# A four-stage Flamingo block on one core: the first slots' 1 / rms taken from their norm's variance, and the contexts' keys and values placed between layer 0's last block and its combinations

## The chip, the cores and the metric

The kernel runs on 1 core of one Trainium2 chip. TensorE (PE) multiplies 128x128 tiles into PSUM, VectorE (DVE) and ScalarE (ACT) do elementwise work and empty PSUM, GpSimd (POOL) does elementwise work on SBUF and issues the indirect DMAs, SyncE (SP) issues most other DMAs. Each engine works through its own instructions in order and waits on semaphores of the others.

The metric is the device time of one execution in microseconds. The kernel before took a median of 1169.84 us in 3 runs (1164.18 to 1171.93).

## The reference, cut to what matters

`x` is 4 x 512 x 256, the context `ctx` as well; all is float32. Four stages add to `x`: local attention with a feed-forward part, a mixture of 8 experts (two for each token), a slot attention against the context, and a second mixture of experts.

```python
x = x + tanh(g_xattn[0]) * aft_local_block(layernorm(x), ctx)
x = x + tanh(g_ffn[0])   * moe0(layernorm(x))          # layer 0 ends here
x = x + tanh(g_xattn[1]) * slot_attention(layernorm(x), ctx)
x = x + tanh(g_ffn[1])   * moe1(layernorm(x))

def layernorm(x, eps=1e-5):                  # mean 0, variance var / (var + eps)
    return (x - mean(x)) / sqrt(var(x) + eps)

def rmsnorm(x, w, eps=1e-6):
    return x * rsqrt(mean(x * x) + eps) * w

def slot_attention(slots, P):
    Pn = rmsnorm(P, input_norm_w)
    k, v = Pn @ Wk.T, Pn @ Wv.T              # once
    for _ in range(3):
        sn = rmsnorm(slots, slot_norm_w)
        scores = (sn @ Wq.T) @ k.T / 16
        attn = softmax(scores, axis=slots)
        attn = attn / (attn.sum(-1) + 1e-6)
        slots = gru_cell(attn @ v, slots)
    return slots
```

The slots of the first of the three iterations are the output of a layernorm without weights. Their mean square, which `rmsnorm` needs, is therefore `var * rs * rs` with the layernorm's own variance and `rs = (var + 1e-5) ** -0.5`.

## The kernel before

A batch is 512 tokens, four tiles (`NT`) of 128; D = 256 is two chunks (`ND`) of 128. A product of a batch with a 256-column weight chunk is a PSUM tile 128x512. Each float32 matmul of the program shows as two matmul instructions in the profile, a transpose as one.

Up to the end of the first iteration the order on PE, DVE, ACT and SP is the order of the code (`manual_schedule` over these engines, opened as `st_o` and closed behind `c1s(B - 1)`); POOL's order, and everything from there to the next such block, is laid out by a scheduler. `PSUM` is cut into four `mm` tiles, two `tr` tiles for transposes and two `tok` tiles.

**Start.** For batch 0 and 1 the code norms the inputs (`in_stats`, `in_apply`), adds the context, turns the sum (`in_turn`: eight transposes, evacuated as `embT`) and computes keys (`keys`: eight 128x512 matmul instructions from `embT`), queries and values. `window_turn()` transposes the position window `pw` and ends with the four transposes of `far`; behind it stand `in_turn(1)`, `more_emb(1)` (on POOL) and `keys(1)`. `spin(n)` (used at the start) multiplies the identity with itself into an `mm` tile that nobody reads: one 128x512 product for each n.

**Layer 0's experts.** `block(s)` runs 19 blocks of sorted rows; the last two are half blocks of 128 rows. Its order is: turn block s+1, `up()` of s, `down()` of s-1. `down()` multiplies `he` with the second weights, DVE copies the result to `yb`, SP stores it to `sorted_y`. After the loop `blocks[-1].down()` finishes the last one, and a branch on `more0` skips blocks that these inputs don't have. Context b is normed by ACT, POOL and DVE inside the loop (`ctx_norm`, `ctx_scale`).

**Hand-over.** `c0g(b)` issues eight indirect gathers (`got` from `sorted_y`) on POOL; `c0x(b, i)` adds the two gathered rows of token tile i to `x` on DVE (`combine`, two operations) and takes its statistics; after the fourth, `power()` computes `ve` on DVE and `rs` on POOL. For contexts 1 to 3: `ctx_turn(b)` (eight transposes; `pT`, one half evacuated by DVE, one by ACT), `ctx_keys(b)` (eight 128x512 matmul instructions; `kT`, one half by DVE, one by ACT), `ctx_values(b)` (two halves of eight 128x256 matmul instructions; the first copied by ACT, the second by DVE into `cs[b]`). The loads of `wih` and `whh` are issued by ACT.

**Slots, first iteration.** `c0n(b)` applies the layernorm (`s0`), `c0s(b)` transposes it (`hT`), `c1a1(b)` squares `hT` on ACT (tile `sq`, one buffer) and adds its two chunks (on DVE through `on_dve`, else on POOL), `c1a2(b)` sums over partitions with four 128x1 products against `ones` and takes the power -1/2 (`rsqrt4`: `ve` on DVE, the power on POOL), `c1b(b)` broadcasts the result by transposing it (`bp`, four transposes) and multiplies: `sn = hT * bp`. `c1s(b)` is scores, exp and division, `c1u1(b, b+1)` the update `u` with the combinations of the next batch between, `c1u2` its transposes, `c2(b)` the GRU: four gates g0 to g3 of eight matmul instructions each, then the new state, with other work called behind the gates.

Of the kernel before, what the change touches and what calls it, by code (L numbers as in the profile page):

```python
# [8 lines left out]
FP = mybir.dt.float32  # L9
# [56 lines left out]
def flamingo_kernel(  # L66
# [19 lines left out]
    def tr_tile():  # L86
        return ps_tr.tile([P, T], FP, tag="tr", name="tr")
# [147 lines left out]
    def rsqrt4(dst, src, mul, eps):  # L235

        ve = small.tile([P, NT], FP, tag="ve", name="ve")
        nc.vector.tensor_scalar(ve, src, mul, eps, ALU.mult, ALU.add)
        nc.gpsimd.tensor_tensor(dst, ve, mhalf, ALU.pow)
# [23 lines left out]
    def spin(n, width=T // P):  # L263

        sp = mm_tile()[:, : width * P]
        for _ in range(n):
            nc.tensor.matmul(
                sp.rearrange("p (a b) -> p a b", b=P), ident,
                ident.unsqueeze(1).to_broadcast([P, width, P]), start=True, stop=True,
            )  # L270
# [590 lines left out]
    def window_turn():  # L861
        def turned(*pairs):
            tp = tr_tile()
            for k, (i, j) in enumerate(pairs):
                nc.tensor.transpose(
                    tp[:, k * P : (k + 1) * P], pw[:, i, j * P : (j + 1) * P], ident
                )
            return tp

        def both(tp):  # L870
            return tp.rearrange("p (j t) -> p j t", j=2)

        act(ew[0][:, 0:2, :EDGE], both(turned((0, 0), (1, 0), (0, 1), (1, 1))))
        act(ew[1][:, 1:3, :EDGE], both(turned((2, 2), (3, 2), (2, 3), (3, 3))))
        tp = turned((1, 2), (2, 1))
        act(ew[0][:, 2, P:EDGE], tp[:, :P])
        act(ew[1][:, 0, :P], tp[:, P : 2 * P])
        tp = tr_tile()
        for i in TILES:
            nc.tensor.transpose(  # L880
                tp[:, i * P : (i + 1) * P], far[:, i : i + 1].to_broadcast([P, P]), ident
            )
        act(base, tp)
# [30 lines left out]
    def in_turn(b):  # L914
        a = A[b]
        embT = a["embT"] = ap.tile([P, ND, T], FP, tag="embT", name="embT")
        if b == 0:
            tps = [tr_tile() for _ in range(ND)]
            for i in TILES:
                if i == 2:  # L920
                    spin(1, 1)
                for c in range(ND):
                    nc.tensor.transpose(
                        tps[c][:, i * P : (i + 1) * P], a["emb"][:, i, c * P : (c + 1) * P],
                        ident,
                    )
            act(embT[:, 0, :], tps[0])
            dve(embT[:, 1, :], tps[1])
            spin(1, 1)
        else:  # L930
            transpose_tokens(embT, a["emb"], act)
# [279 lines left out]
    def ctx_scale(b):  # L1211
        rs = A[b]["rs"]
        for i in TILES:
            nc.vector.tensor_scalar(
                cs[b][:, i, :], cs[b][:, i, :], rs[:, i : i + 1], None, ALU.mult
            )
# [19 lines left out]
    values(0, 1, pool)  # L1236
    in_apply(1)
    window_turn()
    in_turn(1)
    more_emb(1, pool)  # L1240
    keys(1)
# [113 lines left out]
    def ctx_turn(b):  # L1355
        if b < 2:
            pT = ep2.tile([P, ND, T], FP, tag="pT", name="pT", bufs=2)
        else:
            pT = bp2.tile([P, ND, T], FP, tag="xn", name="pT")
        for c in range(ND):  # L1360
            tp = tr_tile()
            for i in TILES:
                nc.tensor.transpose(
                    tp[:, i * P : (i + 1) * P], cs[b][:, i, c * P : (c + 1) * P], ident
                )
            if c == 0:
                nc.vector.tensor_scalar(pT[:, c, :], tp, col("inw", c), None, ALU.mult)
            else:
                nc.scalar.activation(pT[:, c, :], tp, AF.Copy, scale=col("inw", c))
        return pT  # L1370

    def ctx_keys(b, pT):
        kT = kpool.tile([P, ND, T], FP, tag=f"kT{b}", name=f"kT{b}")
        for o in range(ND):
            kp = mm_tile()
            project(kp, [(feat(wkq, c, o), pT[:, c, :]) for c in range(ND)])
            if o == 0:
                nc.vector.tensor_scalar(kT[:, o, :], kp, col("snw", o), None, ALU.mult)
            else:
                nc.scalar.activation(kT[:, o, :], kp, AF.Copy, scale=col("snw", o))  # L1380
        kTs.append(kT)

    def ctx_values(b, pT):

        for g in range(NT // 2):
            vp = tok_tile()
            for k in range(2):
                project(
                    vp[:, k, :],
                    [  # L1390
                        (tokens(pT, c, 2 * g + k), wqkv1_t[:, 2 * ND + c, :])
                        for c in range(ND)
                    ],
                )
            (act, dve)[g](cs[b][:, 2 * g : 2 * g + 2, :], vp)
# [80 lines left out]
    for s in range(TOTAL0):  # L1476
        if s == TOTAL0 - 3:
            more0 = moe0.used(moe0.tab_half, 0)
        if s + AHEAD < TOTAL0:
            load_block(Block(*sure(s + AHEAD)))  # L1480
        block(s, 0, TOTAL0)
        if s == 1:
            moe0.blocks_behind()
        if s == 2:
            moe0.place(0)
        if s in (4, 8, 12):
            ctx_norm(s // 4)
        if s in (6, 10, 14):
            ctx_scale((s - 2) // 4)
    blocks[-1].down()  # L1490
    with tc.If(more0 < E, preferred_fallthrough_block=False):
        others = [(s,) for s in range(SURE0, PAIRS)]
# [27 lines left out]
    def c0x(b, i):  # L1520
        (got, n), norm = G[b][0][i], G[b][1]
        moe0.combine(got, b, i, n)
        norm.stats(xs[b], [i])
        if i == NT - 1:
            norm.power()

    c0g(0)
    pTs = {}
    pTs[1] = ctx_turn(1)
    ctx_keys(1, pTs[1])  # L1530
    ctx_values(1, pTs[1])
    pTs[2] = ctx_turn(2)
    c0x(0, 0)
    ctx_keys(2, pTs[2])
    c0x(0, 1)
    pTs[3] = ctx_turn(3)
    c0x(0, 2)
    ctx_keys(3, pTs[3])
    wih_t = load_w("wih_t", wih, queue=nc.scalar)
    whh_t = load_w("whh_t", whh, queue=nc.scalar)  # L1540
    c0x(0, 3)
    st_b.close()


    with ExitStack() as st_c:
# [4 lines left out]

        def c0n(b):

            s0 = bp1.tile([P, NT, D], FP, tag="xnT", name="s0")
            G[b][1].apply(s0, xs[b])
            G[b] = s0

        def c0s(b):

            if b:
                c0n(b)  # L1560
            s0 = G[b]
            hT = cp.tile([P, ND, T], FP, tag=f"hT{b}", name=f"hT{b}")
            transpose_tokens(hT, s0)
            hTs.append(hT)

        C, S = {}, {}

        def on_dve(b):
            c1a1(b, nc.vector)

        def c1a1(b, mix=nc.gpsimd):

            hT = hTs[b]
            sq = const.tile([P, ND, T], FP, tag="rows", name="sq")
            nc.scalar.activation(sq, hT, AF.Square)
            mix.tensor_tensor(sq[:, 0, :], sq[:, 0, :], sq[:, 1, :], ALU.add)
            S[b] = sq

        def c1a2(b):
            sq = S[b]  # L1580
            sp = tok_tile().rearrange("p a b -> p (a b)")[:, :NT]
            for i in range(NT):
                project(sp[:, i : i + 1], [(tokens(sq, 0, i), ones[:, 0:1])])
            rs = small.tile([P, NT], FP, tag="rs", name="rs")
            rsqrt4(rs, sp, 1.0 / D, 1e-6)
            S[b] = rs

        def c1b(b):

            hT, rs = hTs[b], S[b]  # L1590
            bp = tr_tile()
            for i in range(NT):
                nc.tensor.transpose(  # L1593
                    bp[:, i * P : (i + 1) * P], rs[:, i : i + 1].to_broadcast([P, P]), ident
                )
            sn = cp2.tile([P, ND, T], FP, tag="sn", name="sn")
            for c in range(ND):
                nc.vector.tensor_tensor(sn[:, c, :], hT[:, c, :], bp, ALU.mult)  # L1598
            S[b] = sn
# [396 lines left out]

        order = [b for it in range(ITERS) for b in range(B)]
        c0n(0)
        ctx_values(2, pTs[2])
        c0s(0)  # L2000
        c1a1(0, nc.vector)
        ctx_values(3, pTs[3])
        c1a2(0)
        c0g(1)
        c1b(0)

        adds = []
        for b in range(B - 1):
            c1s(b)
            for fn in adds:  # L2010
                fn()
            adds = []
            c1u2(b, c1u1(b, b + 1))
            c2(
                b, late=adds, g0=[(c0s, b + 1), (on_dve, b + 1)], g1=[(c1a2, b + 1)],
                g2=[(c1b, b + 1)] + ([(c0g, b + 2)] if b + 2 < B else []),
            )
        c1s(B - 1)
# [239 lines left out]
```

## Time and profile before

| | |
|---|---|
| median of 3 runs | 1169.84 us (1164.18 to 1171.93) |
| profiled execution | 1168.72 us, its span 1166.7 us |
| mean granted PE clock | 0.982 of full speed |
| last half block of layer 0 to the first scores of batch 0 | 400.6 to 431.2 us of the span |
| first iteration, batch 0 to the start of batch 3's scores | 431.2 to 554.4 us |
| combination of one tile on DVE (`combine`) | 2 x 480 ns |
| one indirect gather | 953 ns on POOL, 2.8 us to landing |
| power -1/2 of a 128x4 tile on POOL | 1.0 us |

In a timeline row stand: start in us of the span, duration, engine, line, operation, output<-inputs, how many are merged, and in brackets how long the engine had been idle before and what ended that. PE rows are matmuls, PEld rows weight loads. A window row gives the busy time and number of instructions of each engine in a stretch, then the TensorE clock that was granted (1.00 is full speed), the share of the DMA engines and what they moved.

### The profile page before, as it was taken

The numbers are of one execution on the slowest core, as the hardware profiler recorded it, in microseconds if no ns is written. First come the engines' busy times: TensorE is split into PE (matmuls) and PEld (weight loads), VectorE is DVE, ScalarE is ACT, GpSimd is POOL, SyncE is SP. The second block draws the span as 40 slices with busy tenths as digits, with TensorE's granted clock in tenths as the row PEclk, the third lists the DMA queues.
The fourth block names the chain that finished last, engine by engine and source line by source line (L and its number), as shares of the span: only waits on it lengthen the run. The fifth ranks groups of instructions, "written<-read, shape, count | busy, mean of one in ns | idle before, by whom it ended". The sixth has DMA issues, their size and how long they took to land.

```text
span 1166.7 us, 13509 instructions
## 1 busy us (share of the span) xinstructions
PE 1099.1 (94%) x4370; PEld 743.0 (64%) x4370; DVE 628.4 (54%) x1857; ACT 327.9 (28%) x625; POOL 289.2 (25%) x305
## 2 busy tenths in 40 slices
PE   7999999999989989999999999999998998999985
PEld 4757775766778755545555545554655486888874
DVE  7794974673534355644423332333466577666653
ACT  3132213131234223333324332433322222222211
POOL 5100113122300141441201211121131425433422
PEclk9999999999999999999999999999999999999998
DMA  9999401000178430110599200000010464867764
GB/s 318 370 340 342 163 1 50 23 4 33 57 234 265 158 105 17 34 36 1 123 215 214 55 0 1 1 1 0 1 38 9 153 220 148 271 199 250 246 209 149
DMA packets 122956, 147.41 MB, mean 126 GB/s; under 512 B 15076, under 2 KB 98082, under 8 KB 122880
## 3 DMA queue, kind: packets, MB, share of 16 engines
q1 hardware_dynamic: 114032, 127.25, 36.7%
q0 software_dynamic: 8160, 17.61, 4.5%
q10 hardware_dynamic: 688, 1.62, 0.4%
q8 instruction: 37, 0.61, 0.2%
q14 instruction: 39, 0.32, 0.1%
HBM read 76.74 MB, written 74.54 MB: 130 GB/s over the span
## 4 chain that ended last, share of the span: by engine, by line
PE 37%; DVE 11%; issue 6%; POOL 4%; DMA 3%; ACT 3%; POOLq 0%; ACTq 0%; DVEq 0%
PE mm L285 26%; PE tok L285 9%; DMA acc<-sorted_x,there 3%; POOL hT L1674 1%; POOL hT L1673 1%; PE tr L277 1%; DVE nb L1619 1%; POOL acc L1943 1%; DVE hT L1677 1%; ACT ex L1622 1%; DVE n L1693 1%; DVE x L744 1%; DVE vs L1610 1%; ACT n L1694 1%; DVE xn L254 1%
## 5 line engine op out<-in xcount | busy, mean ns | idle before, releaser
L285 PE MATMUL mm<-hT,whh_t 128*128 128x512 f32 x288 | 138.8, 601 | 0.0
L285 PE MATMUL mm<-uT,wih_t 128*128 128x512 f32 x288 | 135.7, 593 | 0.0
L285 PE MATMUL mm<-xT,gu 128*128 128x256 f32 (+1 forms) x672 | 132.1, 355 | 0.7 <-ACT xT L719 0.7
L285 PEld LDWEIGHTS mm<-xT,gu 128*128 128x128 f32 x672 | 115.7, 191 | 14.3 <-ACT xT L719 0.9
L285 PE MATMUL tok<-vs,ex 128*128 128x257 f32 x384 | 96.8, 398 | 12.4 <-DVE vs L1610 10.2
L285 PEld LDWEIGHTS mm<-uT,wih_t 128*128 128x128 f32 x288 | 54.5, 191 | 66.8 <-issue 65.6
L285 PEld LDWEIGHTS tok<-vs,ex 128*128 128x128 f32 x384 | 71.6, 195 | 38.7 <-ACT ex L1622 13.7
L285 PE MATMUL mm<-sn,kT 128*128 128x512 f32 x192 | 87.7, 611 | 1.6 <-DVE sn L1598 1.6
L285 PEld LDWEIGHTS mm<-hT,whh_t 128*128 128x128 f32 x288 | 52.7, 192 | 51.1 <-issue 50.8
L1926 ACT ACTIVATE sl<-mm,bias 128x256 f32<-128x256 f32 (+1 forms) x84 | 37.5, 448 | 158.1 <-PE mm L285 129.1
L285 PE MATMUL tok<-dn,h 128*128 128x256 f32 x296 | 71.5, 390 | 9.5 <-DVE h L1927 5.0
L824 POOL TENSOR_TENSOR rs<-ve,mhalf 128x4 f32<-128x4 f32 (+1 forms) x25 | 28.3, 1133 | 202.4 <-DVE ve L821 177.4
L285 PEld LDWEIGHTS mm<-sn,kT 128*128 128x128 f32 x192 | 37.6, 197 | 48.9 <-issue 39.8
L1673 POOL TENSOR_TENSOR hT<-hT,n 128x512 f32<-128x512 f32 x18 | 22.8, 1268 | 181.7 <-ACT n L1694 181.7
L285 PEld LDWEIGHTS tok<-dn,h 128*128 128x128 f32 x296 | 54.7, 194 | 20.1 <-DVE h L1927 8.6
L1988 POOL DMA_INDIRECT out<-acc,ids x37 | 37.8, 1022 | 98.5 <-DVE acc L1984 77.6
L1665 ACT ACTIVATE rz<-mm,brz 128x512 f32<-128x512 f32 x48 | 33.0, 687 | 96.0 <-PE mm L285 93.2
L1927 DVE SCALAR_TENSOR_TENSOR h<-mm,bias,sl 128x256 f32<-128x256 f32 (+1 forms) x84 | 37.7, 450 | 39.2 <-ACT sl L1926 37.7
L285 PE MATMUL mm<-aT,w_t 128*128 128x512 f32 x128 | 57.9, 609 | 0.9 <-ACT aT L1090 0.9
L285 PE MATMUL tok<-w_t,h1T 128*128 128x256 f32 x256 | 56.0, 379 | 0.0
L285 PEld LDWEIGHTS tok<-w_t,h1T 128*128 128x128 f32 x256 | 48.4, 190 | 6.9 <-issue 0.5
L1598 DVE TENSOR_TENSOR sn<-hT,tr 128x512 f32<-128x512 f32 x24 | 15.4, 683 | 64.0 <-PE tr L1593 64.0
(337 smaller groups left out, 1794.9 us busy)
## 6 DMA issues: line engine op xcount, KB each, us to landing
sorted_x<-zero SPq DMA_DIRECT2D x16, 1060.0 KB, 21.4
sorted_x<-zero SPq DMA_DIRECT2D x16, 1024.0 KB, 10.5
sorted_y<-zero SPq DMA_DIRECT2D x16, 1024.0 KB, 11.2
gu<-in_gate_w SPq DMA_DIRECT2D x21, 512.0 KB, 4.4
gu<-in_up_w SPq DMA_DIRECT2D x21, 512.0 KB, 5.6
dn<-in_down_w SPq DMA_DIRECT2D x21, 512.0 KB, 5.5
w<-in_w_stack SPq DMA_DIRECT2D x38, 256.0 KB, 3.6
xb<-sorted_x SPq DMA_DIRECT2D x17, 256.0 KB, 3.9
```

Source lines behind the costliest of these rows:

```text
L254: nc.vector.tensor_scalar(dst[:, i, :], src[:, i, :D], mean[:, i : i + 1], rs[:, i : i + 1], ALU.subtract, ALU.mult,)
L277: nc.tensor.transpose(tp[:, i * P : (i + 1) * P], src[:, i, c * P : (c + 1) * P], ident)
L285: nc.tensor.matmul(acc, lhsT, rhs, start=(k == 0), stop=(k == len(pairs) - 1))
L744: nc.vector.scalar_tensor_tensor(acc, got[:, 2 * n + k, :], self.w[b][:, k, i : i + 1], acc, ALU.mult, ALU.add,)
L824: pool.tensor_tensor(self.rs[:, part], self.ve[:, part], mhalf[:, part], ALU.pow)
L1598: nc.vector.tensor_tensor(sn[:, c, :], hT[:, c, :], bp, ALU.mult)
L1610: nc.vector.tensor_scalar(vs[:, j, 0:D], v[:, j, :], vs[:, j, D : D + 1], None, ALU.mult)
L1665: nc.scalar.activation(rz[:, g, :], gp, AF.Sigmoid, bias=brz[:, g : g + 1])
L1673: mix.tensor_tensor(h, h, n, ALU.subtract)
L1926: nc.scalar.activation(sl, hp[:, 0, :], AF.Silu, bias=bias[:, 0, f : f + 1])
L1927: nc.vector.scalar_tensor_tensor(self.h[:, f, :], hp[:, 1, :], bias[:, 1, f : f + 1], sl, ALU.add, ALU.mult)
L1988: ins = nc.gpsimd.indirect_dma_start(out=tokens_out, out_offset=bass.IndirectOffsetOnAxis(ap=self.ids[:, k : k + 1], axis=0), in_=acc[:, k ...
```

## The change

One product of the identity is put ahead of `in_turn(1)`. `ctx_turn(1)` moves from behind the branch to between the last two `down()`. The turns, keys and values of contexts 1 to 3 and the four combinations of batch 0 get a new order, and `ctx_values` can do one half at a time. In the first iteration the sum of squares is no longer computed: `c0n` takes 1 / rms from the layernorm's variance and `rs` (two products, `ve` and the power on 128x4 tiles). For batch 0, `c0first` broadcasts that before it transposes the slots, copies the broadcast to SBUF (`by`) and forms `sn` from the transposes in PSUM. For the other batches `c1a1` and `c1a2` fall away from g0 and g1 of the GRU before; `c1b` stays. Iterations 2 and 3 compute the sums as before.

```diff
     window_turn()
+    spin(1)
     in_turn(1)
...
-    def ctx_values(b, pT):
-
-        for g in range(NT // 2):
+    def ctx_values(b, pT, halves=range(NT // 2)):
+
+        for g in halves:
...
+    pTs = {1: ctx_turn(1)}
     blocks[-1].down()
     with tc.If(more0 < E, preferred_fallthrough_block=False):
...
     c0g(0)
-    pTs = {}
-    pTs[1] = ctx_turn(1)
     ctx_keys(1, pTs[1])
+    pTs[2] = ctx_turn(2)
     ctx_values(1, pTs[1])
-    pTs[2] = ctx_turn(2)
     c0x(0, 0)
     ctx_keys(2, pTs[2])
     c0x(0, 1)
     pTs[3] = ctx_turn(3)
     c0x(0, 2)
+    ctx_values(2, pTs[2])
+    c0x(0, 3)
     ctx_keys(3, pTs[3])
     wih_t = load_w("wih_t", wih, queue=nc.scalar)
     whh_t = load_w("whh_t", whh, queue=nc.scalar)
-    c0x(0, 3)
...
         def c0n(b):
+            norm = G[b][1]
+            q = small.tile([P, NT], FP, tag="q", name="q", bufs=2)
+            nc.vector.tensor_tensor(q, norm.mv[:, :, 1], norm.rs, ALU.mult)
+            nc.vector.tensor_tensor(q, q, norm.rs, ALU.mult)
+            rs = small.tile([P, NT], FP, tag="rs", name="rs")
+            rsqrt4(rs, q, 1.0, 1e-6)
+            S[b] = rs
             s0 = bp1.tile([P, NT, D], FP, tag="xnT", name="s0")
-            G[b][1].apply(s0, xs[b])
+            norm.apply(s0, xs[b])
             G[b] = s0
+        def c0first():
+            bp = tr_tile()
+            for i in range(NT):
+                nc.tensor.transpose(
+                    bp[:, i * P : (i + 1) * P], S[0][:, i : i + 1].to_broadcast([P, P]), ident
+                )
+            by = bp2.tile([P, T], FP, tag="relu", name="by")
+            act(by, bp)
+            hT = cp.tile([P, ND, T], FP, tag="hT0", name="hT0")
+            hTs.append(hT)
+            sn = cp2.tile([P, ND, T], FP, tag="sn", name="sn")
+            for c in range(ND):
+                tp = tr_tile()
+                for i in range(NT):
+                    nc.tensor.transpose(
+                        tp[:, i * P : (i + 1) * P], G[0][:, i, c * P : (c + 1) * P], ident
+                    )
+                nc.vector.tensor_tensor(sn[:, c, :], tp, by, ALU.mult)
+                act(hT[:, c, :], tp)
+            S[0] = sn
         def c0s(b):
-            if b:
-                c0n(b)
+            c0n(b)
...
-        def on_dve(b):
-            c1a1(b, nc.vector)
...
         c0n(0)
-        ctx_values(2, pTs[2])
-        c0s(0)
-        c1a1(0, nc.vector)
-        ctx_values(3, pTs[3])
-        c1a2(0)
+        ctx_values(3, pTs[3], [0])
+        c0first()
+        ctx_values(3, pTs[3], [1])
         c0g(1)
-        c1b(0)
...
             c2(
-                b, late=adds, g0=[(c0s, b + 1), (on_dve, b + 1)], g1=[(c1a2, b + 1)],
+                b, late=adds, g0=[(c0s, b + 1)],
                 g2=[(c1b, b + 1)] + ([(c0g, b + 2)] if b + 2 < B else []),
             )
```

## The prediction

> **What bounds the kernel now.** First the page: TensorE (PE) is busy for nearly the whole span, so only what changes its waits, its work or its clock can change the time.
>
> ```profile
> span 1166.7 us, 13509 instructions
> PE 1099.1 (94%) x4370; PEld 743.0 (64%) x4370; DVE 628.4 (54%) x1857; ACT 327.9 (28%) x625; POOL 289.2 (25%) x305
> ```
>
> The diff touches three stretches, so next the timeline of PE alone around the hand-over from layer 0 to layer 1 (start, us, engine, line, output<-inputs, count, the idle time before it and what ended it).
>
> ```profile
> 397.63 2.23 PE L285 MATMUL tok<-w,he 128*128 128x256 f32 x8
> 400.62 1.07 PE L1363 MATMUL tr<-ident,c 128*128 128x128 f32 x8 [0.76 <-PEq L1491]
> 402.09 3.70 PE L285 MATMUL mm<-pT,wkq 128*128 128x512 f32 x8 [0.41 <-DVE pT L1367]
> ...
> 427.38 0.95 PE L285 MATMUL tok<-ones,sq 128*128 128x1 f32 x8
> 429.73 0.65 PE L1593 MATMUL tr<-ident,rs 128*128 128x128 f32 x4 [1.41 <-POOL rs L239]
> 431.16 8.82 PE L285 MATMUL mm<-sn,kT 128*128 128x512 f32 x16 [0.78 <-DVE sn L1598]
> ```
>
> From 400.62 (first context transposes) to 431.16 (first scores) 30.5 us pass. Starts in the same timeline give the paces: 8 transposes 0.86 (453.64 to 454.51), 8 matmuls 128x512 3.44 (450.20 to 453.64), 16 matmuls 128x256 3.45 (405.63 to 409.08), 8 of 128x1 0.81 (457.95 to 458.76). The work of the stretch is, of the contexts 1 to 3, keys 10.3, values 10.3 and turns 2.6, slots' transposes 0.9, sums of squares 0.9, broadcast 0.4: 25.4. So 5.1 us are waits. And the 16 score matmuls, which take 6.87 in the next batch (473.01 to 479.88), take 8.66 here (431.16 to 439.82). Why, the windows view says (span, then busy us and instructions by engine, granted PE clock, DMA share, GB/s); I read it at both places where the diff takes away PE idle time.
>
> ```profile
> 24.00:26.60 2.60, 0.65 (x4) 0.41 (x4) 2.60 (x6) 1.25 (x4) 1.39 (x2) 1.00 1.07 364
> 26.60:28.60 2.00, 1.66 (x8) 0.94 (x8) 0.92 (x3) 0.59 (x2) 0.17 (x1) 0.95 1.12 334
> 28.60:30.00 1.40, 1.36 (x2) 0.84 (x3) 0.00 (x0) 0.48 (x1) 1.40 (x1) 0.50 1.10 347
> 30.00:32.00 2.00, 2.00 (x3) 0.68 (x2) 0.00 (x0) 0.00 (x0) 0.77 (x1) 0.54 1.10 346
> ...
> 427.00:431.00 4.00, 1.98 (x15) 1.60 (x13) 1.51 (x4) 0.00 (x0) 2.03 (x2) 1.00 0.00 0
> 431.00:433.00 2.00, 1.84 (x2) 0.84 (x3) 0.70 (x2) 0.00 (x0) 1.51 (x2) 0.55 0.32 84
> 433.00:434.50 1.50, 1.50 (x3) 0.67 (x2) 0.00 (x0) 0.00 (x0) 1.20 (x2) 0.50 0.35 117
> ```
>
> Behind each thinly used stretch PE gets half its clock for some 3.4 us, and the next four matmuls run at 0.86 instead of 0.43: 1.7 us each time.
>
> **A, spin(1) before in_turn(1).** PE is idle 1.63 us until 26.66 (waiting for DVE's emb), then has eight transposes paced by DVE, then keys(1) at half clock from 28.64 to 32.03. The spin is one 128x512 product, two matmuls, 0.86 us; it runs from about 25.0 to 25.9, inside that idle time, and delays nothing: its PSUM buffer was last used by keys(0), long evacuated. The 3.4 us from 25.0 to 28.4 then hold 1.7 us of work at the paces above instead of 0.85 (eight transposes). The 3.4 us from 7.9 on hold 1.7 (eight transposes, four matmuls of spin's 128x128, one 128x512) and kept the clock; those from 134.2 on hold 1.2 and kept it too, those from 813.5 on 1.3 and lost it, those from 171.8 on 0.8 and lost it: the limit is near 1.25. Gain: four matmuls, 1.7. Between 33.7 and 50 PE has no wait over 0.7, and up to 326 none on a DMA, so it is passed on. Bounds: 0 if the clock falls all the same, 1.7.
>
> **B, the hand-over.** (1) ctx_turn(1) now stands between the last two down() of layer 0. There PE waited 0.47 for DVE's he, so eight transposes (0.86) delay the last down by 0.4, and the first work behind the branch from 400.62 to 401.03; but that is now ctx_keys(1) itself, which started at 402.09. pT is ready: DVE evacuates it (0.75) between the two yb copies, ACT (0.69) in idle time. The last yb store slips on DVE by 0.4, but SP issued it only at 401.6, when the store before it had landed, and yb would be there at 400.7; so the gathers' start (404.47) doesn't move. What the branch itself costs (0.76) stays.
> (2) PE's queue is then keys 1, turn 2, values 1, keys 2, turn 3, values 2, keys 3, half of values 3, broadcast, slots' transposes, other half. Each evacuation now has a product to hide under, so the waits for pT (0.41, 0.57, 0.62 ahead of the three keys) go. Work: 3 keys 10.3, 2 turns 1.7, 3 values 10.3, broadcast 0.4, slots 0.9 = 23.6. From 401.03 that ends at 424.7 without waits.
> (3) The waits that replace the old ones. The gathers are issued 1.26 apart and land 2.8 later, the eighth at 416.2. On DVE the fourth combination stands behind values 2's copy: PE ends values 2 at 416.5, the copy runs to 417.4, the combination and its statistics (1.0+0.43+0.18) to 419.0, ve, POOL's power (1.05) to 420.3. New on DVE ahead of the four applies: q, q, ve, three 128x4 operations at 0.18 (as rd L1641 and L1642 follow each other at 448.65 and 448.81), 0.55; applies (1.38) to 422.3; beside them POOL's second power (1.01, row rs L239) to 422.0. PE has finished half of values 3 at 421.7, so the broadcast waits 0.4; the second block of slots' transposes needs the broadcast's PSUM buffer, which ACT's copy (0.58) frees: 0.4 more. Half of values 3 (1.7) covers DVE's two sn products (0.69 each). Scores start at 424.7+0.8 = 425.5 instead of 431.16: 5.7. Without the wait before, the clock stays up: 1.8 more. B is 7.5. Bounds: 4 (DVE 2 us later than I queue it, clock lost) and 8.3 (no wait at all).
> c0g(1)'s gathers come some 3 us earlier, now behind POOL's power, and batch 1's last lands near 438.5; its combination ran at 448.9, now 441.4. wih and whh move behind keys 3 on ACT, some 1 us later; they landed at 426 and are needed after 442.
>
> **C, the other three batches and iteration 2.** Each g1 loses ACT's square (1.06), DVE's sum (0.69) and eight matmuls 128x1.
>
> ```profile
> 457.95 0.95 PE L285 MATMUL tok<-ones,sq 128*128 128x1 f32 x8
> 458.76 1.96 PE L285 MATMUL mm<-hT,whh_t 128*128 128x512 f32 x4
> ...
> 537.24 1.88 PE L285 MATMUL mm<-uT,wih_t 128*128 128x512 f32 x4
> 539.24 1.05 PE L285 MATMUL tok<-ones,sq 128*128 128x1 f32 x8
> 540.15 1.96 PE L285 MATMUL mm<-hT,whh_t 128*128 128x512 f32 x4
> ```
>
> Batch 1 saves 0.8; batches 2 and 3, where PE also waited for the sums, 1.2 each (538.96, the end of the products before, to 540.15). q, q, ve delay the applies by 0.55: before they ended at 453.29 and the last transpose of the first four starts at 453.97, so no wait is made, by 0.1.
> What takes their place: in the changed program's order the squares of iteration 2 move up. Batch 0's stands on ACT between exp and u in batch 1's turn: u is 0.75 late, PE 0.5, but the last u waits for DVE's rd, which c0x sets, so nothing is passed on. Batch 1's stands between the third and fourth u of batch 2's turn, and its tile, single, is read by PE's sums behind the third u (529.3 to 530.1): square to 531.3, u to 531.8, PE's transposes at 531.8 instead of 530.61. That costs 1.2. In return the last batch's scores (554 to 571) lose eight 128x1 matmuls and a square that stood ahead of the last exp (562.32): 1.0. C: 0.8+1.2+1.2-1.2+1.0 = 3.0. Bounds 1.5 and 4.2.
>
> **The sum.** 1.7+7.5+3.0 = 12.2. The profiled run took 1168.7 (span 1166.7 and 2.0 around it), 1.1 under the median of the three (1169.84). So 1156.5 by the profile, 1157.6 by the median; I say 1157.
>
> **Rivals.**
> *The clock doesn't pay.* 3.5 of the 12.2 are two half-clock stretches. The clock falls in this profile at nine places before the end, and where it does depends on how the work lies in time; if the timed runs lose it at other places instead, 8.7 are left: 1160. For: the same kernel's runs spread from 1164.18 to 1171.93, more than its work can explain. Against: at both places idle time and transposes fill so much that most positions of a 3.4 us stretch are thin.
> [...]
> *The chain to the first sn.* Gathers, four combinations, power, q, power is now covered by only half of values 3. If DVE is 2 us later than queued above, PE waits that long and, with an idle stretch that thin, the clock goes too: 12.2-2-1.8 = 8.4, 1160.
> *Slower.* The first gather waited 24.19 us "until PE mm L285", an event at 404.1, by the profile. Its wait may be for a PE product behind the branch, whose place the change alters. If it had to wait for keys 3 (420.0), the gathers would land at 431.7, the combination end at 433.3, the applies at 436.6, scores start near 439.5 at half clock: 8.3 lost where 7.5 was to be gained, against A and C's 4.7: 3.6 slower, 1173. It turns the gain into a loss from a gather start of about 416 on (3.6 us earlier). Against: the last store's landing (403.55) explains the start as well, and the event belongs to keys 1, which come earlier.
>
> **Chances.** Forecast 0.60 (own range 1153 to 1160, from the bounds and the spread of a median); clock 0.24 and chain 0.12 (1157 to 1163); slower 0.04. 0.8 of it: 1152.5 to 1162.5. Over 1% faster is below 1158.1 (1% is about what a measurement of this kernel can tell): three quarters of the first case and a fifth of the next two, 0.52; within 1% 0.45; slower by over 1% 0.03.
>
> **What would show it.** Right: clock 1.00 at 26 to 32 and through the first scores; scores some 5.7+1.7 earlier; PE waits before the broadcast of 0.2 to 0.8; turns of batches 1 and 2 shorter by 0.8 and 1.2; a new wait of about 1.2 for u in batch 2's. Wrong: idle PE over 1.5 us before the broadcast, the gathers later than 404.5 less A, half clock at either place, or the gain of 408 lost again before 600.

## The result, and the profile after

The changed kernel took a median of 1162.42 us in 7 runs (1157.39 to 1164.09); beside them the kernel before took 1169.84 (7 runs, 1164.18 to 1171.93). The ratio is 0.993, with a 95% interval of 0.9906 to 0.9954. Two later comparisons, each on a chip of its own, gave 0.9897 (0.9873 to 0.9921) and 0.9922 (0.9888 to 0.9956). In microseconds of 1169.84 the three are 8.2, 12.0 and 9.1; their mean is 9.8, where 12.2 was forecast.

The page of the changed kernel says that the share of PE is the same, in a shorter span:

```profile
span 1160.2 us, 13466 instructions
PE 1098.6 (95%) x4340; PEld 742.3 (64%) x4340; DVE 624.8 (54%) x1860; ACT 324.9 (28%) x623; POOL 290.3 (25%) x305
```

The timeline of PE at the hand-over, changed kernel:

```profile
401.26 1.03 PE L285 MATMUL tok<-w,he 128*128 128x256 f32 x4
402.13 1.04 PE L1364 MATMUL tr<-ident,c 128*128 128x128 f32 x8
403.00 1.03 PE L285 MATMUL tok<-w,he 128*128 128x256 f32 x4
404.83 3.67 PE L285 MATMUL mm<-pT,wkq 128*128 128x512 f32 x8 [0.81 <-DVEq L1493]
...
426.23 0.65 PE L1570 MATMUL tr<-ident,rs 128*128 128x128 f32 x4 [0.47 <-POOL rs L239]
...
427.60 0.66 PE L1581 MATMUL tr<-ident,s 128*128 128x128 f32 x4 [0.28 <-ACT by L1574]
...
429.82 7.03 PE L285 MATMUL mm<-sn,kT 128*128 128x512 f32 x16
436.69 0.60 PE L285 MATMUL tok<-vs,ex 128*128 128x257 f32 x2
```

Before, the last two `down()` (they stand in one row) began at 397.63 and the first scores at 431.16, 33.5 later; now it is 401.26 (the context's transposes stand between the two) and 429.82, 28.6 later. From here on "last `down()`" in a stretch means the start of these two. The two waits that were forecast are there, 0.47 for POOL's `rs` and 0.28 for ACT's `by`. But the last two `down()` themselves begin 3.6 later than before, in a stretch where the diff changes nothing.

The windows view of the changed kernel at the places where the clock was looked at, and at a new one (columns as before: the granted clock is the third number from the right):

```profile
26.50:28.50 2.00, 1.99 (x9) 0.77 (x8) 1.65 (x5) 0.59 (x1) 0.00 (x0) 1.00 1.12 330
28.50:30.00 1.50, 1.20 (x7) 0.71 (x6) 0.00 (x0) 1.07 (x2) 0.95 (x1) 1.00 1.10 347
30.00:33.00 3.00, 3.00 (x8) 1.33 (x7) 1.01 (x3) 0.54 (x1) 1.40 (x1) 1.00 1.10 346
...
430.00:432.00 2.00, 2.00 (x6) 0.81 (x6) 1.03 (x3) 0.00 (x0) 0.34 (x1) 1.00 0.01 3
432.00:436.70 4.70, 4.70 (x13) 2.07 (x12) 3.17 (x10) 2.17 (x6) 3.53 (x4) 1.00 0.29 84
...
524.00:528.00 4.00, 2.43 (x19) 2.10 (x18) 3.76 (x11) 2.01 (x3) 1.39 (x2) 1.00 0.00 0
528.00:531.50 3.50, 3.50 (x6) 1.40 (x5) 2.23 (x9) 0.00 (x0) 2.71 (x3) 0.52 0.00 0
```

Keys of batch 1 and the first scores now have the full clock. The half clock at 528 is new; the stretch before it holds only 2.43 of PE in 4.00. The timeline of PE and that of ACT there:

```profile
523.99 0.49 PE L277 MATMUL tr<-ident,u 128*128 128x128 f32 x3
524.32 0.95 PE L285 MATMUL tok<-ones,sq 128*128 128x1 f32 x8
526.84 0.77 PE L277 MATMUL tr<-ident,u 128*128 128x128 f32 x5 [1.57 <-ACT u L1670]
```

```profile
525.37 1.06 ACT L1602 ACTIVATE sq<-hT 128x1024 f32<-128x1024 f32 x1 [1.56 <-PE tok L285]
526.33 0.46 ACT L1670 ACTIVATE u<-tok,rd 128x256 f32<-128x256 f32 x1
```

This is the wait forecast in C. ACT may write the next batch's square only when PE has read the last one (`tok<-ones,sq`), the fourth `u` stands behind the square, and PE waits 1.57 for it, at a place where it waited 1.19 for `u` before. The timeline of PE there in the kernel before:

```profile
528.93 0.49 PE L277 MATMUL tr<-ident,u 128*128 128x128 f32 x3
530.61 0.77 PE L277 MATMUL tr<-ident,u 128*128 128x128 f32 x5 [1.19 <-ACT u L1643]
```

From the start of the first three transposes of `u` to that of the last five 1.68 passed before and 2.85 now, so the wait costs 1.17, as forecast (1.2).

By stages the two profiled executions differ as follows (starts and stretches from the timelines of PE; low places are stretches of 3.41 us at a granted clock of 0.5, those at the very end left out; the first weigh is the first product of `ew`, at 33.74 before and 32.80 now, and the first `tok<-vs,ex` of a batch is its first u product):

| stretch | before | after |
|---|---|---|
| keys of batch 1: first transpose to first weigh | 7.08, 1 low | 5.52 |
| first weigh to the start of the last `down()` | 363.9, 2 low | 368.5, 5 low |
| last `down()` to the first scores | 33.5 | 28.6 |
| first scores to the first `tok<-vs,ex` | 8.66, 1 low | 6.87 |
| from there to the same of iteration 2's first | 143.6, 1 low | 141.1, 1 low |

The second row loses a part of what the other rows gain: it is 4.6 us longer with the same work and three low places more.

### The profile page after: what moved, and what is told of

Read it like the earlier page. It is cut to its first block, busy times and chain, and to the rows that moved or that the text cites. A ratio compares the mean times of both kernels' runs of the same rounds, so it can differ in the third digit from the quotient of the medians.

```text
span 1160.2 us, 13466 instructions
## 1 busy us (share of the span) xinstructions
PE 1098.6 (95%) x4340; PEld 742.3 (64%) x4340; DVE 624.8 (54%) x1860; ACT 324.9 (28%) x623; POOL 290.3 (25%) x305
## 4 chain that ended last, share of the span: by engine, by line
PE 36%; DVE 11%; issue 7%; POOL 5%; DMA 3%; ACT 2%; POOLq 0%; ACTq 0%; DVEq 0%
PE mm L285 25%; PE tok L285 9%; DMA acc<-sorted_x,there 3%; POOL acc L1970 1%; PE tr L277 1%; DVE nb L1646 1%; POOL hT L1701 1%; POOL hT L1700 1%; ACT ex L1649 1%; DVE n L1720 1%; DVE hT L1704 1%; ACT n L1721 1%; DVE vs L1637 1%; DVE xn L254 1%; DVE x L744 1%
## 5 line engine op out<-in xcount | busy, mean ns | idle before, releaser
L285 PE MATMUL mm<-sn,kT 128*128 128x512 f32 x192 | 84.5, 593 | 0.8 <-DVE sn L1625 0.8
L285 PEld LDWEIGHTS mm<-sn,kT 128*128 128x128 f32 x192 | 36.4, 190 | 46.0 <-issue 38.9
```

The lines of the kernel that those rows point to most:

```text
L285: nc.tensor.matmul(acc, lhsT, rhs, start=(k == 0), stop=(k == len(pairs) - 1))
```

## The experiments

**The spin alone.** The kernel before with

```diff
     window_turn()
+    spin(1)
     in_turn(1)
```

> The kernel before with spin(1) alone. Theory: the places of half clock depend on how the program's work happens to fall on a grid of 3.41 us, which lies differently in each execution, so each execution draws its own; a low place costs 1.7 us, and the spin takes away one thin place that nearly every position of the grid would hit. Then: keys of batch 1 (first transpose to first weigh) 5.4 to 5.6 instead of 7.08, at clock 1.00; first weigh to the last down() is 360.2 + 1.7 for each low place in it, whatever their number is this time; the rest of the program as before; time 1.6 faster, which a ratio of 0.9986 inside an interval that holds 1 would say. Rival: the spin itself costs the 4.6 us that the changed kernel lost between first weigh and the last down(): then that stretch is 368 here too, and without more than two low places in it; time 3 us slower. Rival: the half clock of 28.4 to 31.8 has nothing to do with how much PE does there: then keys take 7.08 as before.

Its timeline of PE:

```profile
25.53 1.02 PE L267 MATMUL mm<-ident 128*128 128x512 f32 x2
27.12 1.68 PE L277 MATMUL tr<-ident,emb 128*128 128x128 f32 x8 [0.57 <-DVE emb L910]
29.09 3.70 PE L285 MATMUL mm<-embT,wqkvo_t 128*128 128x512 f32 x8 [0.30 <-ACT embT L280]
```

Keys of batch 1 took 5.51 from first transpose to first weigh, at the full clock. First weigh to the start of the last `down()` took 368.1 with four low places, against 367.0 by 360.2 + 4 x 1.7. The stretch was long here too, but with four low places, where the rival that the spin itself costs the time allowed no more than two; whether it is the spin that brings them, the repeats below say. Time: 0.998 (0.9951 to 1.0008), nothing that can be told.

**The order alone.** Contexts and combinations in the new order, `ctx_turn(1)` moved, but the sums of squares as before and no spin. Against the changed kernel:

```diff
         c0n(0)
         ctx_values(3, pTs[3], [0])
-        c0first()
+        c0s(0)
+        c1a1(0, nc.vector)
         ctx_values(3, pTs[3], [1])
+        c1a2(0)
         c0g(1)
+        c1b(0)
```

> The changed order of contexts and combinations alone (ctx_turn(1) between the last two down(), turns ahead of values, values 2 behind the third combination, values 3 in two halves), with the old sums of squares for the first 1 / rms and in the loop, and no spin. Theory: the order by itself saves the three waits for pT (0.41, 0.57, 0.62) and half a turn, about 2.5, and gives back about 1.7, since the squares and their sums of batch 0 have only half of values 3 to hide under: last down() to the first u product 42.19 before, here 40.5 to 42 with one low place in it (PE waits over 1 us remain before the sums and the broadcast), 38.8 to 40.3 without. The batch turns as before (40.1, 40.7). Time 1 faster, not to be told from before. Rival (the two parts of the hand-over add up, and the order is most of the 6.8): 36 to 38.

Its timeline of PE:

```profile
426.77 1.89 PE L285 MATMUL tok<-wqkv_t,pT 128*128 128x256 f32 x8
429.76 1.02 PE L285 MATMUL tok<-ones,sq 128*128 128x1 f32 x8 [1.10 <-DVE sq L1577]
432.19 0.65 PE L1594 MATMUL tr<-ident,rs 128*128 128x128 f32 x4 [1.41 <-POOL rs L239]
433.62 6.62 PE L285 MATMUL mm<-sn,kT 128*128 128x512 f32 x8 [0.78 <-DVE sn L1599]
```

From the last `down()` to the first u product it took 41.95, with two low places in a row behind these waits (scores to u product 9.89, 3.0 more than at the full clock). Without the clock that is 38.9, against 40.4 before (42.19 less 1.79): the order by itself is worth 1.5 here. Ratio 0.9992 (0.9972 to 1.0013).

**1 / rms from the variance alone.** The order of before, no spin. Against the kernel before:

```diff
         ctx_values(2, pTs[2])
-        c0s(0)
-        c1a1(0, nc.vector)
+        c0first()
         ctx_values(3, pTs[3])
-        c1a2(0)
         c0g(1)
-        c1b(0)
```

and the same `c0n` and the same calls in the loop as in the changed kernel.

> 1 / rms from the variance alone, for all four batches, with the order of contexts and combinations of before, and no spin. Theory: at the hand-over it saves the sums (0.81) and the waits of 1.41 and 0.78, since values 2 lies ahead of the broadcast and values 3 behind it: 42.19 to about 39 with a low place in the scores, 37.4 without one. Together with the order alone (about 1) less than the 6.8 of both: the order pays in full only with the shorter chain. Batch 1's turn 0.9 shorter, batch 2's 1.0, batch 3's not shorter, since the square's wait for PE's sums delays the fourth u by 1.2 (a wait of about 1.6 ahead of the transposes of u), longer by 1.7 where the clock falls behind it; last scores 0.8 shorter. Time 5 to 7 faster, ratio about 0.995. Rival (parts add up): 36 or less at the hand-over if the order alone gives less than 1, and the loop's saving the whole 3.0.

```profile
428.78 0.65 PE L1569 MATMUL tr<-ident,rs 128*128 128x128 f32 x4 [0.53 <-POOL rs L239]
...
430.15 0.66 PE L1580 MATMUL tr<-ident,s 128*128 128x128 f32 x4 [0.28 <-ACT by L1573]
430.64 3.62 PE L285 MATMUL tok<-wqkv_t,pT 128*128 128x256 f32 x16
434.10 6.17 PE L285 MATMUL mm<-sn,kT 128*128 128x512 f32 x14
```

This is its timeline of PE: the waits of 1.41 and 0.78 are gone, 0.53 and 0.28 have come, and the scores follow the values with no low place. Last `down()` to the first u product: 38.12 (37.4 was expected). That is 2.3 under the 40.4. Order 1.5 and variance 2.3 make 3.8; both together make 5.0 (40.4 to 35.43), so 1.2 comes only from the two together. The batch turns (from the first u product of one batch to that of the next) are those of the changed kernel, 39.16, 39.73 and 42.33, the half clock behind the wait for `u` included (at 532.2). Ratio 0.9967 (0.9939 to 0.9994), 3.9 us where 5 to 7 were expected.

**The same two kernels once more.** No edit.

> The kernel before once more, for a second look at its clock. Theory (a free grid of 3.41 us, and half clock for the stretch of it that follows one filled less than about 0.38): the low places will not all be those of the first look (28.4, 175.2, 250.3, 431.2, 574.5, 816.9, 888.6, 902.2, 1127.5); with the grid at another phase some of them go and others come (9, 132, 174 twice, 294, 324, 972), all of them behind thin stretches, and first weigh to the last down() is 360.2 + 1.7 for each low place in it. Rival (the clock falls at fixed places of the program): the same nine places within 0.5 us, 363.9 again.

> The changed kernel once more. Theory: low places differ from those of its first look (9.3, 173 twice, 251.6, 299.4, 330.1, 528.1, 811.4, 883.1, 896.7 twice, 1122.0), and the stretch from first weigh to the last down() differs from 368.46 by 1.7 for each place more or fewer; what does not hang on the clock comes again to 0.1: keys 1 start 3.57 behind the last down(), waits of 0.47 and 0.28 at the broadcast, 1.57 ahead of the transposes of u in batch 2's turn. Ratio to before 0.991 to 0.996. Rival (fixed places): 368.4 again, with all places as they were.

The kernel before had low places at 27.9, 174.7 (two in a row), 253.2, 301.0, 324.8, 437.5, 580.8, 823.2, 908.5, 976.8, 993.9 and 1133.8 (two). From first weigh to the last `down()` there were five, not two, and it took 369.4, not 363.9; 360.2 + 5 x 1.7 is 368.7. One product shows it, `shared_in(3)`: the timeline of PE in the first execution, and then that in the second.

```profile
296.30 2.22 PE L285 MATMUL tok<-rw,xnT 128*128 128x8 f32 x16 [0.24 <-ACT xnT L280]
298.38 7.11 PE L285 MATMUL mm<-xnT,ws 128*128 128x512 f32 x16
```

```profile
297.99 2.22 PE L285 MATMUL tok<-rw,xnT 128*128 128x8 f32 x16 [0.24 <-ACT xnT L280]
300.06 8.81 PE L285 MATMUL mm<-xnT,ws 128*128 128x512 f32 x16
```

The program is the same, what stands ahead of it is the same, and its sixteen matmuls take 1.70 more. So the places are not fixed, and the spin isn't needed for a stretch of 369. That it is the execution and not only the chip, the runs of the third comparison show: of 19 executions of the kernel before on one chip, the one with the lowest mean granted clock (0.973) took 1175.78 us, and the three with the highest (0.985) 1163.97 to 1164.83. The changed kernel, once more, had again five low places there (172.5 twice, 251.0, 298.8, 322.7; one of them elsewhere than at first) and 369.4; what does not hang on the clock came again: keys 1 3.44 behind the last `down()` (3.57 at first), 28.4 from the last `down()` to the scores, 1.57 ahead of the transposes of `u`, turns of 39.16 and 39.73. The ratio, 0.9897, is a little below the range given, 0.991 to 0.996.

**The spin taken out of the changed kernel, beside the changed kernel.**

> The changed kernel, beside the next two on one chip. Theory: the work that the change takes off the path is the same each time (hand-over 32.9 to 33.1 from the last down() to the first u product, turns 39.16, 39.73, 42.3), 7.4 in all, and what the clock adds or takes differs from execution to execution; ratio to before between 0.990 and 0.994. Rival (its ratios of 0.993 and 0.9897 were two different gains on two chips): outside 0.989 to 0.995.

> The changed kernel without spin(1). Theory: half clock in the keys of batch 1 is a matter of the grid's phase and comes in most executions without the spin (three of four so far) and in none with it (six so far): keys of batch 1 5.5 to 7.1 here, first transpose to first weigh, 6.4 in the mean; the spin is worth about 1, less than the 1.7 forecast and less than can be told by time: 0 to 2 us over the changed kernel. Rival (the spin is worth its 1.7 each time): 7.08 here. Rival (it is worth nothing): 5.5 here, and no low place within 24 to 32.

Without the spin, the timeline of PE:

```profile
26.93 2.02 PE L277 MATMUL tr<-ident,emb 128*128 128x128 f32 x8 [1.26 <-DVE emb L910]
28.91 4.99 PE L285 MATMUL mm<-embT,wqkvo_t 128*128 128x512 f32 x8
```

6.80 from first transpose to first weigh, with a low place at 28.1. The changed kernel beside it had 5.52 and hand-over and turns as before (28.57, 39.17, 39.73, 42.33); its ratio, 0.9922, is inside the range given. Without the spin the ratio is 0.9941 (0.9914 to 0.9968), and the medians are 2.1 us apart (1161.43 and 1159.29); the intervals overlap, so the time doesn't tell what the spin is worth. Of the five traces of kernels without the spin four have a low place there, and the stretch took 7.08, 6.74, 6.42, 5.52 and 6.80, 6.51 in the mean; with it none of eight has one, and all show 5.51 or 5.52.

**The sum of squares in a tile of its own.** The changed kernel with

```diff
             nc.scalar.activation(sq, hT, AF.Square)
-            mix.tensor_tensor(sq[:, 0, :], sq[:, 0, :], sq[:, 1, :], ALU.add)
-            S[b] = sq
+            sm = const.tile([P, T], FP, tag="sqs", name="sm")
+            mix.tensor_tensor(sm, sq[:, 0, :], sq[:, 1, :], ALU.add)
+            S[b] = sm
```

and the products against `ones` read `sm`. It ran three times:

> The changed kernel, and the sum of the two squares goes to a tile of its own, so that the single square tile is held until the sum is taken and not until PE has read it. Theory: what batch 3's turn lost (33.83 before to 35.48 from the first u product of batch 2 to the first sn,kT product) is the square's wait for PE's sums and the low clock that the wait's thin stretch brings: here the stretch is 32.3 to 32.8, the wait ahead of the transposes of u 0.9 to 1.1 instead of 1.57, no low place within 524 to 532; the rest as in the changed kernel; time 1.2 to 2.9 under it, ratio to before 0.990 to 0.992. Rival (the wait is for something else, u or rd itself): the wait stays at 1.5 and the stretch at 33.8 or more; time as the changed kernel.

> The changed kernel with the sum of squares in a tile of its own, once more and timed in more rounds. What does not hang on the clock comes again: no wait ahead of the transposes of u in batch 2's turn, the four and a half later batch turns 38.06 and not 38.52. These make 1.57 + 5 x 0.46 = 3.9 against the changed kernel, and 1.7 more where the clock fell behind the wait at 528: ratio to before 0.988 to 0.992. Rival (its first time was low because its clock fell less by chance): 0.992 or more.

> The changed kernel with the sum of squares in a tile of its own, on the same chip as the changed kernel. Theory: turns 39.16, 39.73, 39.67 (42.3 before it) and 38.06 in place of 38.52: 2.6 + 5 x 0.46 = 4.9, less what the clock gives back, so 3 to 6 us under the changed kernel. Rival (no difference, as the medians 1163.46 and 1163.78 on one chip say): within 1.5 us.

Its timelines of PE and ACT at the place of the new wait:

```profile
521.05 0.49 PE L277 MATMUL tr<-ident,u 128*128 128x128 f32 x3
521.38 0.95 PE L285 MATMUL tok<-ones,sm 128*128 128x1 f32 x8
522.32 0.76 PE L277 MATMUL tr<-ident,u 128*128 128x128 f32 x5
```

```profile
516.00 1.06 ACT L1602 ACTIVATE sq<-hT 128x1024 f32<-128x1024 f32 x1 [1.82 <-DVE hT L1705]
516.96 0.45 ACT L1671 ACTIVATE u<-tok,rd 128x256 f32<-128x256 f32 x1
```

The square now stands ahead of the four `u`, not between the third and the fourth, and PE does not wait for `u` at all; 0.9 to 1.1 was expected to be left. The third turn (first u product of batch 2 to that of batch 3) is 39.67 in all three traces, where the changed kernel has 42.33 with the half clock, and 40.64 in the kernel without the spin, whose clock fell elsewhere. From the first u product of batch 2 to the last batch's scores it is 32.8, at the upper end of what was expected. In iteration 2 the square has moved one exp forward, and four turns are 38.06 instead of 38.52. The whole first iteration (first u product to that of iteration 2) takes 138.6 in two traces and 140.3, with a low place at 570, in the third, instead of 141.1; the next six turns take 227.8 instead of 229.6. In time: 0.9893 (0.9862 to 0.9924), 0.9867 (0.9843 to 0.9892) and 0.9909 (0.9876 to 0.9942), in the two sessions that timed the changed kernel too it is under it both times, by 0.0030 and 0.0013 (medians 1163.46 to 1163.78, and 1157.35 to 1159.29). The first two ratios are lower than expected, and the last difference, 1.9, lies between the two theories. The work saved is shown; that the time follows is likely, but no interval excludes that it doesn't. Against the kernel before it is faster by about 1%.

**Throwaway products in the thin stretches.** The last kernel with five more calls: `spin(1)` ahead of `moe_turn(1)`, ahead of `moe_turn(2)` and between `c1u2(3, u)` and `d0b1(2, act)`, `spin(2)` ahead of the first `blocks[0].turn()`, and

```diff
+                spin(4)
                 others()
```

> The kernel with the sum of squares in a tile of its own, and nine throwaway products of 128x512 more (0.86 us each, 7.7 of added work on PE) in the thin stretches that every trace so far shows: one ahead of moe_turn(1), one ahead of moe_turn(2), two ahead of the first block's turn, one between c1u2(3) and d0b1(2), four ahead of the late blocks' branch. Theory: they stand where PE waits anyway (0.43, 0.43, 1.65, 0.98, 4.47), so the work costs 1 to 1.5 us, and takes away the low places behind these stretches, 3 to 5 in an execution at 1.7: time 4 to 6 us under the kernel without them, ratio to before 0.984 to 0.987; no low places near 174, 250, 329, 890 and 1108. Rival (the granted clock does not follow what PE does there): low places stay and the time is 1 to 3 us more.

The gain did not come: 0.9872 (0.9847 to 0.9897) beside 0.9867 without them. Nor did most of the low places go: behind the targets they stood at 174.5, 249.6 and 1123.4, and only that near 890 was gone (near 329 this chip's traces have none, with the products or without). Three of the places were read wrongly. Ahead of the late blocks, in its timeline of PE, and then in that of the same session without the products:

```profile
1114.26 0.38 PE L715 MATMUL tr<-ident,xn 128*128 128x128 f32 x2
1114.48 3.60 PE L267 MATMUL mm<-ident 128*128 128x512 f32 x8
1122.05 2.48 PE L285 MATMUL tok<-dn,h 128*128 128x256 f32 x8 [3.98 <-issue]
```

```profile
1122.35 2.67 PE L285 MATMUL tok<-dn,h 128*128 128x256 f32 x7 [4.59 <-issue]
```

Without them PE stood 4.59 at that branch; with 3.44 of products it stood 3.98 behind them. In the twelve traces without them it is 3.90 to 4.59, so nothing shows that they hid any of it; it looks as if the wait at this branch starts when PE gets there. And the thin stretch near 172 is made by the sixteen 128x8 products: PE counts as busy for 2.2 us with them, but the low place behind stayed (174.5), although the spin in front of it ran; so did that behind the next such products (249.6). Ahead of the first block, at last, PE had nothing to wait for on this chip, since it had waited earlier (last section), and two products more simply took 1.7. Two low places in a row near 174 became one, and 8 were left where the same session's trace without the products has 11. But the other two traces without them have 7 and 10, so this one doesn't show that the products kept the clock; the 7.7 us of work bought nothing that the time shows.

## Why the prediction came out as it did

The first median, 1162.42, is inside the range (1152.5 to 1162.5) by only 0.08. It is above the forecast's own 1153 to 1160 and among the times of its two milder rivals, and a gain of under 1% had been given 0.45, less than the 0.52 of a larger one. Where one median falls in so wide a spread is luck: by the mean gain of 9.8 it would be 1160.0. The mechanism of each step was seen; most of the sizes were too large. Term by term, from the stretches above:

| step | forecast | measured |
|---|---|---|
| A: keys of batch 1 at full clock | 1.7 | 1.0 (6.51 to 5.52, means) |
| B: order and waits, to the first scores | 5.7 | 5.0 (33.53 to 28.56) |
| B: clock in the first scores | 1.8 | 2.3 (9.18, mean of four traces; 6.87) |
| C: three turns, without the clock | 3.0 | 2.7 (142.06 to 141.09 less 1.7) |
| C: clock behind the new wait | 0 | -0.4 (1.7 x (3/4 - 5/5)) |
| sum | 12.2 | 10.6 |

The sum lies between the three timed gains, 8.2, 9.1 and 12.0.

**A** was "four matmuls, 1.7", each time. In these traces a low place follows a thin stretch of the 3.41 us grid on which the clock changes (last section), and without the spin the grid still missed it in one trace of five; also, when the low place comes early, part of it falls on transposes that wait for `emb` anyway (26.5 in the kernel with the order alone, 6.42). So it is 1.0 in the mean. The limit "near 1.25" did not follow from its rows, of which 1.2 kept the clock and 1.3 lost it; thirteen traces show a band from 1.2 to 1.4 in which both happen (last section). The spin, with 1.7, is clear of it.

**B**, order and waits: keys 1 began 3.57 behind the last `down()` (forecast 3.40), and from there to the scores 24.99 passed (24.5). The waits named are the right ones, 0.47 and 0.28 for 0.4 and 0.4; the rest is a tenth here and there between groups that the sum of the paces doesn't hold. One reading was wrong: the 0.47 that PE was to have waited for the last `down()` is the idle time of the weight loads (`[0.47 <-DVE he L1178]` in PEld's row at 398.72); PE's matmuls began there only 0.23 later than their pace, so the transposes hide under less of it. The 33.53 is the first execution's. In the second, on the chip of the second comparison, it was 34.52, since PE waited 1.61 for the third context's `pT`, where it had waited 0.62 (415.88):

```profile
422.34 3.70 PE L285 MATMUL mm<-pT,wkq 128*128 128x512 f32 x8 [1.61 <-DVE pT L1367]
```

The changed kernel has no wait ahead of these keys in any of its traces, so B was worth about 6 there, and part of that comparison's 12.0 may be this; one trace doesn't say how often it happens. The parts are worth 1.5 and 2.3 alone, so the step was right to cost them as one: the order pays where the shorter chain lets half of values 3 cover it. Without its waits the hand-over kept the clock in all nine traces of kernels with the variance's 1 / rms, and lost it in all four with the old sums.

**C**: batch 1's turn gained 0.9 (forecast 0.8), batch 2's 1.0 (1.2), batch 3's with the last scores 0.9 (1.0). The wait ahead of the fourth `u` was forecast, and costed at 1.2; what the step missed is that this wait makes a thin stretch of its own. All five traces of kernels with it have one low place in this part, four of them right behind the wait (527.5 to 532.2); with the old sums three of four have one, at 575 to 581. So the change moved it rather than took it away (the -0.4 of the table, from so few traces, can't be told from nothing), and where A and B were given the clock, C should have been charged with it.

**The sum** was made against one execution, and this was the other thing that was off, though it moves only the first pair of profiles. That execution had two low places between first weigh and the last `down()`; all the other traces of these kernels and their parts have three to five. Its span was therefore some 5 us shorter there than usual, and the first pair of traces shows a gain of 6.5 where the work and the means give 10.6.

**The rivals.** "The clock doesn't pay" gave 8.7. It was right that the clock falls elsewhere in another execution, and wrong that nothing is left: at both places where idle time was taken out, the low place was gone in every trace. By the table the clock paid 2.9 of its 3.5, and the rest 7.7 of its 8.7. By the number this rival was still the nearer one: the mean gain of 9.8 is 1.1 from its 8.7 and 2.4 from the 12.2. A low place of these traces doesn't need a long gap of PE ahead of it: the one at 528 stands behind a gap of 1.57. "The chain to the first `sn`" did not come in seven of the eight traces with the new hand-over, where PE waited 0.47 or 0.48 for it. In the eighth, the kernel without the spin, it came in part:

```profile
427.24 0.65 PE L1569 MATMUL tr<-ident,rs 128*128 128x128 f32 x4 [1.02 <-POOL rs L239]
```

The first gather started there 9.4 behind the last `down()`, and 7.1 to 7.2 behind it in the seven (6.8 and 7.1 in the kernel before); what made it late was not tried. In none of them did the gathers wait for later keys.

## What to carry to other kernels

When a change takes a wait out of one place, look for the stretch in which its replacement waits, and charge the clock there too (here 1.57 ahead of the fourth `u`, and the half clock at 528 behind it). Where a stretch gets half its clock only in some executions (keys of batch 1 without the spin in four of five), cost it by means over several executions, and compare pairs of profiles by stretches with the low places counted out. Look for a single tile that two engines hand on: here ACT's square waited 1.56 for PE's sums, the fourth `u` stood behind it in ACT's queue, and PE waited 1.57 for that; giving the sum its own tile cost 2 KB in each partition and shortened two stretches by 2.5 and 1.8 us, the clock behind the wait included.

## What the runs showed of the hardware

**The clock goes by a grid in these traces.** The low places have a granted clock of 0.50 and are 3.41 us long or a multiple of it (28.41 to 31.82 in the kernel before; 173.12 to 179.95, two in a row, in the changed kernel), and their starts in one trace lie multiples of 3.413 us apart (28.41 and 175.18 in the kernel before: 43 x 3.413). From execution to execution the grid lies differently against the work: counted from the start of the span it begins at 1.10 in the first trace of the kernel before and at 2.45 in that of the changed kernel. PE's work in a stretch can be counted by columns at the full pace (0.43 us for 512, from the 3.44 of eight matmuls). The eight transposes from 25.0 on in the kernel before then fill 0.25 of their stretch, and the one ahead of the low place at 528.1 in the changed kernel is filled to 0.35; from 134.2 on, in the kernel before, it is 0.36, and the clock was kept. In the 13 traces every stretch at the full clock that was filled less than 0.36, so counted, was followed by a low one, and none filled over 0.40; between lies a mixed band (in the first trace of the kernel before 0.37 from 885.2 on lost the clock, and 0.39 from 294.7 on kept it). These are counts in these traces, not more. (The first stretch of a trace, which begins in products still at half pace, eight in 4.73 us instead of 3.44 in the kernel before, and the last 12 us are left out.) Products of 128x8 then fill nearly nothing, although PE is shown busy: the sixteen from 173.21 on in the kernel before are 2.32 us of busy PE and count 0.11. A low stretch goes by the same count: those that their work, at half the pace, filled up to 0.77, which is 0.38 at the full pace, were followed by a second low one (two in a row at 433 in the kernel with the spin alone; 0.34 in the one from 173.1 on in the changed kernel), and those filled from 0.80 on by one at the full clock (0.84 in the one from 574.5 on in the kernel before).

**A wait that one chip has and another doesn't.** On the chip of the second comparison, where the kernel before took 1177.76 in the median and not 1169, ACT and DVE stood still before they emptied the first context's turn. DVE's row there in the changed kernel, and then the same in its first execution:

```profile
321.11 0.75 DVE L1368 TENSOR_SCALAR pT<-tr,col_t 128x512 f32<-128x512 f32 x1 [3.48 <-remote]
```

```profile
318.98 0.75 DVE L1368 TENSOR_SCALAR pT<-tr,col_t 128x512 f32<-128x512 f32 x1 [0.61 <-PE tr L1364]
```

All four traces from that chip have it, 3.48 to 3.59, and none of the others. What DVE waited for was not tried.
